# A state-space scan beside a mixture of experts: GpSimd adds the sums of two steps in every second pair of steps of blocks 1 to 4, and TensorE sums four states at once there

## The chip, the core and the metric

The kernel runs on one core of a Trainium2 chip. Its time is the device time of one execution in microseconds (us); for the kernel before the change it is 1565.81 us, the median of three runs. A core has a matrix engine (TensorE, PE in the profile, with PEld for its weight loads), three engines for element-wise work (VectorE or DVE, ScalarE or ACT, GpSimd or POOL), an engine that here issues the transfers (SyncE, SP), and 16 DMA engines. Each engine takes its own instructions in the order in which the program gives them, and waits at an instruction until the semaphores that it needs have come.

## The reference

`x` has 2 sequences of 2048 tokens of 256 channels. It is layer-normed (`xn`), and the output is `x + s * g`:

- `s` is a Mamba layer with residual, then an MLP with residual. Of `xn` (rms-normed) an input projection makes `xp` and `z`, 512 channels each; a causal convolution over 4 tokens and a silu make `xc`; `dt = softplus(...)`, `B` and `C` (16 values per token each) are projections of it. Then the scan over the tokens, for each of 512 channels and 16 states:

```python
def step(h, ts):
    dt_t, B_t, C_t, u_t = ts
    dA = jnp.exp(dt_t[..., None] * A)
    h = h * dA + (dt_t * u_t)[..., None] * B_t[:, None, :]
    y = jnp.einsum('bds,bs->bd', h, C_t)
    return (h, y)
```

  and `(y + xc * D) * silu(z)` goes through the output projection.
- `g` is the silu of a mixture of experts: a gate picks 2 of 8 experts for each token, each expert is 256 to 1024 (relu) to 256.

The change is in the `einsum`: for every channel and token, the 16 products `h * C` are summed over the states.

## The kernel before

Everything is in 32-bit floats. The 4096 tokens are cut into 8 blocks of 512 (`T`), four to a sequence; the 512 channels into 4 groups `d` of 128 partitions; the 16 states into 8 pairs `g`. One **step** `n` (0 to 255, `at[n] = (c, d, g)`, so block `c` is `n // 32` and pair `g` is `n % 8`) does two states of one channel group of one block:

- ScalarE makes `da`, the two exponentials of `dt` times A, two steps ahead (`exps`, L1238).
- VectorE multiplies `du` by the pair's B (L1345) and runs two scans along the 512 tokens (L1349) into the tile `h`, 128 x 2 x 512, one of five buffers. At the first pair of a group it makes `du` (L1342).
- ScalarE saves the last token's state for the next block (`save`, L1275), one step later.
- GpSimd multiplies `h` by the pair's C in place, both states in one instruction of 1024 elements a partition (`times_c`, L1279). For nearly all steps (`paired`) it then adds the second state to the first (L1281).
- TensorE sums over the states: `accumulate` multiplies the identity by the 128 x 512 tile and adds it into the PSUM tile `y` of the channel group (L1251). A `paired` step needs one such matmul, others two. The first matmul of a group adds `xc * D` by a diagonal matrix (L1247). A matmul of 32-bit floats appears as two records in the profile. After the last pair VectorE multiplies `y` by the gate (`gated`, L1259).

The order of all this is written out by hand. In the loop of step `n` the scan of `n` is followed by `save` and `times_c` of `n - 1`, the exponentials of `n + 2`, then `sums(n - LAG)` with `LAG` 3, which calls `accumulate`. After that comes `draw(HALF + owed)`: it takes pieces of other work from lists, until 2.0 us of TensorE time by the planner's own costs (0.86 for a matmul of 512 columns) are given out, twice in each step. The sums are not counted in it. The other work is: the expert and MLP tiles (`Ffn.run`: matmuls L854 and L866, transposes L844, activation L954 on ScalarE, sum L966 on VectorE), the front of the next block (`front`: projections L557, L602, L621, convolution L567 to L582), the gate projection (L708) and the output projection (`out_proj`, L762). In blocks 1 to 4 these are expert tiles.

Inside `front` lies the chain that makes the next block's `dt`, for two channel groups at a time, twice per block: matmuls L621, five activations on ScalarE (L629 to L635), one subtraction on GpSimd (L636), a logarithm on ScalarE (L643), then a subtraction and an add on GpSimd (L648, L649). Beside the first logarithm, `root` makes the norm factors of an earlier block: GpSimd L800, ScalarE L802 and L803, GpSimd L227 to L230. All of these stand in the engines' ordinary queues between the steps' own instructions.

Of the kernel before, what the change touches and what calls it, by code (L numbers as in the profile page):

```python
# [11 lines left out]
ALU = mybir.AluOpType  # L12
# [37 lines left out]
def kernel(  # L50
# [18 lines left out]
    nc = tc.nc  # L69
# [303 lines left out]
    def ring(tag, bufs):  # L373

        n = take(tag)
        later.free(tag, n - bufs)
        return tag, n
# [818 lines left out]
    hs, ys, y_n, hts, das, dus = {}, {}, {}, {}, {}, {}  # L1196
# [45 lines left out]
    def accumulate(n):  # L1242
        c, d, g = at[n]
        if g == 0:
            y_n[c, d] = ring("y", 1)
            ys[c, d] = ps_1.tile([P, T], F32, tag="y", name=f"y{c}_{d}")
            nc.tensor.matmul(ys[c, d], ddiag[:, d, :], xcs[c, d], start=True, stop=False)  # L1247
            skips[0] += 1
        nq = 1 if paired(n) else 2
        for q in range(nq):  # L1250
            nc.tensor.matmul(  # L1251
                ys[c, d], ident, hts[n][:, q, :], start=False,
                stop=(g == DS // 2 - 1 and q == nq - 1),
            )
        if g == DS // 2 - 1:
            y, sz, twice = ys[c, d], szs[c, d], 1.0 if d else 0.5

            def gated():
                nc.vector.scalar_tensor_tensor(sz, y, twice, sz, ALU.mult, ALU.mult)  # L1259
                y_made.add((c, d))  # L1260

            later.put(gated, y_n[c, d], after=2)

    def sums(n):

        g = at[n][2]
        if g:
            if g == 1:
                accumulate(n - 1)
            accumulate(n)  # L1270
# [6 lines left out]
    def times_c(n):  # L1277
        c, d, g = at[n]
        nc.gpsimd.tensor_tensor(hts[n], hts[n], bct[c, "C", g], ALU.mult)  # L1279
        if paired(n):  # L1280
            nc.gpsimd.tensor_tensor(hts[n][:, 0, :], hts[n][:, 0, :], hts[n][:, 1, :], ALU.add)  # L1281

    def paired(n):

        return n >= 8 and not (n >= 190 and n % 2 == 0)
# [34 lines left out]
    for n in range(NS):  # L1320
# [15 lines left out]
        for q in range(2):  # L1336
# [17 lines left out]
            if q == 0 and n > 0:  # L1354
                save(n - 1)
                times_c(n - 1)
# [9 lines left out]
            owed = draw(HALF + owed)  # L1366
    save(NS - 1)
    times_c(NS - 1)
    for n in range(NS - LAG, NS):
        sums(n)  # L1370
# [63 lines left out]
```

## Time and profile before

| | |
|---|---|
| runs | 1567.42, 1560.62, 1565.81 us, median 1565.81 |
| the profiled execution | 1572.91 us, of which span 1571.2 us |
| granted TensorE clock, mean | 0.94 |
| TensorE matmul busy | 1401.4 us, 89% of the span |
| VectorE busy | 1247.6 us, 79% |
| GpSimd busy | 1157.2 us, 74% |
| ScalarE busy | 920.1 us, 59% |
| step 32 starts (its multiply by B, L1345) | 280.7 us |
| step 160 starts | 946.7 us |
| sums L1251 | 594 matmul records, median 592 ns |

The profile shows one execution. A busy time is the time in which an engine runs its instructions. The time in which it stands idle before an instruction is put down to what released that instruction. A group line gives line, engine, operation, the tiles written and read, shapes and count, then busy time and mean duration, then idle time before and who ended it. A timeline line gives start, duration, engine, line, operation and count. "L" is a line of the kernel as printed above. Busy time of TensorE is modelled with overlapping matmuls, so the distance between starts says more of its pace than the duration does.

### The profile page before, as it was taken

To read this page: it belongs to the slowest core of one execution; us is meant where nothing else is said; L and a number is where in the kernel's file an instruction comes from. 1 tells how busy PE (TensorE), PEld (TensorE's weight loads), DVE (VectorE), ACT (ScalarE), POOL (GpSimd) and SP (SyncE) were. 2 spreads that over 40 slices of the span, in tenths; PEclk is the share of its full clock that TensorE was granted. 3 is DMA by queue.
4 is the path that set the end of the run, shared out by engine and by line. 5 is a ranking of instruction groups with operands and counts; after the bars stand their busy time and mean duration, and the time that the engine had idled before them with its cause. 6 is when DMAs were issued, how large, how long until landed. Compare 5 with 4: busy or idle time off the path is not lost. (4 is left out here: it accounts for less than half of the span.)

```text
span 1571.2 us, 18477 instructions
## 1 busy us (share of the span) xinstructions
PE 1401.4 (89%) x5246; PEld 985.5 (63%) x5246; DVE 1247.6 (79%) x1362; ACT 920.1 (59%) x1890; POOL 1157.2 (74%) x775
## 2 busy tenths in 40 slices
PE   5745999998999999999999999999898898799767
PEld 3532667765776667667776777667555565567536
DVE  7458898798778977799879777996898696899952
ACT  4735576567655755477657665675566564374423
POOL 2668589867886689679967887688866768677852
PEclk8557999999999999999999999999999989899988
DMA  5576335923494347724763368245832437645312
GB/s 190 187 258 252 111 120 182 327 91 102 141 321 146 96 131 250 256 88 132 234 255 110 118 213 295 87 127 180 314 105 87 143 101 249 214 131 164 96 59 84
DMA packets 203749, 265.17 MB, mean 169 GB/s; under 512 B 21744, under 2 KB 174192, under 8 KB 203648
## 3 DMA queue, kind: packets, MB, share of 16 engines
q1 hardware_dynamic: 197504, 247.21, 48.0%
q0 software_dynamic: 6144, 16.79, 3.2%
q8 instruction: 42, 0.69, 0.2%
q14 instruction: 59, 0.48, 0.1%
HBM read 227.50 MB, written 36.44 MB: 168 GB/s over the span
## 5 line engine op out<-in xcount | busy, mean ns | idle before, releaser
L1279 POOL TENSOR_TENSOR h<-h,C 128x1024 f32<-128x1024 f32 x256 | 609.9, 2384 | 246.3 <-ACT hs L1275 193.9
L1349 DVE TENSOR_TENSOR_SCAN h<-da,hs,b 128x512 f32<-128x512 f32 x384 | 479.7, 1271 | 42.6 <-PE y L1251 17.2
L1238 ACT ACTIVATE da<-dt,a_neg 128x512 f32<-128x512 f32 x512 | 358.0, 718 | 40.3 <-DVE h L1349 39.7
L1251 PE MATMUL y<-h,ident 128*128 128x512 f32 x594 | 304.6, 615 | 30.6 <-POOL h L1279 20.2
L1345 DVE TENSOR_TENSOR b<-du,B 128x1024 f32<-128x1024 f32 x256 | 314.8, 1230 | 18.0 <-DMA B<-bcd 11.1
L854 PE MATMUL phe<-xsTe,w_e 128*128 128x256 f32 x1248 | 290.4, 384 | 12.5 <-ACT hide L954 8.8
L1281 POOL TENSOR_TENSOR h<-h 128x512 f32<-128x512 f32 x215 | 277.9, 1292 | 16.9
L854 PEld LDWEIGHTS phe<-xsTe,w_e 128*128 128x128 f32 x1248 | 238.7, 192 | 80.6 <-issue 26.3
L866 PE MATMUL poe<-w_e,hide 128*128 128x256 f32 x1248 | 288.7, 380 | 0.0
L866 PEld LDWEIGHTS poe<-w_e,hide 128*128 128x128 f32 x1248 | 235.7, 190 | 64.9 <-issue 33.6
L954 ACT ACTIVATE hide<-phe,b 128x256 f32<-128x256 f32 x312 | 129.3, 469 | 128.9 <-PE phe L854 128.7
L1251 PEld LDWEIGHTS y<-h,ident 128*128 128x128 f32 x594 | 113.0, 197 | 119.6 <-issue 63.3
L1349 DVE TENSOR_TENSOR_SCAN h<-da,b 128x512 f32<-128x512 f32 x128 | 151.3, 1211 | 11.1 <-PE y L1251 3.2
L854 PE MATMUL phm<-xsTm,w_m 128*128 128x256 f32 x512 | 130.9, 410 | 22.7 <-DVE hidm L1015 19.9
L854 PEld LDWEIGHTS phm<-xsTm,w_m 128*128 128x128 f32 x512 | 104.1, 205 | 55.0 <-DVE hidm L1015 24.2
L866 PE MATMUL pom<-w_m,hidm 128*128 128x256 f32 x512 | 119.0, 384 | 2.0 <-DVE xom L1086 1.7
L866 PEld LDWEIGHTS pom<-w_m,hidm 128*128 128x128 f32 x512 | 97.7, 193 | 28.6 <-issue 11.0
L459 POOL DMA_INDIRECT xs_d<-xt,slot x64 | 63.9, 998 | 49.8 <-issue 22.2
L1275 ACT COPY hs<-h 128x2 f32<-128x2 f32 x192 | 36.1, 188 | 94.7 <-DVE h L1349 92.3
L1042 POOL DMA_INDIRECT ykm<-ys_d,row_y x64 | 61.4, 960 | 38.9 <-issue 11.7
L1015 DVE SCALAR_TENSOR_TENSOR hidm<-hidm,phm 128x512 f32<-128x512 f32 x64 | 42.7, 671 | 55.6 <-ACT hidm L1013 55.6
L582 DVE SCALAR_TENSOR_TENSOR xc<-px,par_sb,xc 128x512 f32<-128x512 f32 x96 | 71.5, 747 | 17.2 <-ACT xc L574 11.8
(175 smaller groups left out, 1431.6 us busy)
## 6 DMA issues: line engine op xcount, KB each, us to landing
w_e<-in_w SPq DMA_DIRECT2D x312, 256.0 KB
B<-bcd SPq DMA_DIRECT2D x64, 512.0 KB
C<-bcd SPq DMA_DIRECT2D x64, 512.0 KB
w_m<-in_mlp_w1T SPq DMA_DIRECT2D x64, 256.0 KB
w_m<-in_mlp_w2T SPq DMA_DIRECT2D x64, 256.0 KB
xs<-xs_d SPq DMA_DIRECT2D x39, 256.0 KB
ys_d<-ys SPq DMA_DIRECT2D x39, 256.0 KB
b<-in_b SPq DMA_DIRECT2D x39, 128.0 KB
```

Of the source, the lines that this page charges most:

```text
L459: r = nc.gpsimd.indirect_dma_start(out=xs_d, out_offset=bass.IndirectOffsetOnAxis(ap=slot[:, k, i : i + 1], axis=0), in_=x_of(i // J, i % ...
L582: nc.vector.scalar_tensor_tensor(v[:, s : s + T], px, conv_w[:, d, KC - 1 - s : KC - s], v[:, s : s + T], ALU.mult, ALU.add,)
L854: nc.tensor.matmul(ph[:, q, :], self.w1[c0 // 2][:, k, ts(q, P)], self.xT[:, k, :], start=(k == 0), stop=(k == KM - 1),)
L866: nc.tensor.matmul(po[:, j, :], self.hid[c // 2][:, c % 2, ts(j, P)], self.w2[c // 2][:, c % 2, :], start=(c == 0 and j == 0), stop=(c == ...
L954: nc.scalar.activation(hc[:, q, :], ph[:, q, :], AF.Relu, bias=self.b1[:, c0 + q : c0 + q + 1])
L1042: nc.gpsimd.indirect_dma_start(out=yk[k][:, j, :], out_offset=None, in_=ys_d, in_offset=bass.IndirectOffsetOnAxis(ap=row_y[:, k, i0 + j : ...
L1238: nc.scalar.activation(das[n][:, q, :], dts[c, d], AF.Exp, scale=a_neg[:, d, 2 * g + q : 2 * g + q + 1])
L1251: nc.tensor.matmul(ys[c, d], ident, hts[n][:, q, :], start=False, stop=(g == DS // 2 - 1 and q == nq - 1),)
L1279: nc.gpsimd.tensor_tensor(hts[n], hts[n], bct[c, "C", g], ALU.mult)
L1281: nc.gpsimd.tensor_tensor(hts[n][:, 0, :], hts[n][:, 0, :], hts[n][:, 1, :], ALU.add)
L1345: nc.vector.tensor_tensor(inp, dus[c, d].unsqueeze(1).to_broadcast([P, 2, T]), bct[c, "B", g], ALU.mult,)
L1349: nc.vector.tensor_tensor_scan(hts[n][:, q, :], das[n][:, q, :], inp[:, q, :], 0.0 if c % CPB == 0 else hs[c - 1][:, d, 2 * g + q : 2 * g ...
```

## The change

In steps 32 to 159 (blocks 1 to 4) with `n % 4 == 3`, GpSimd gets one more add of 128 x 512: the pair sum of step `n - 1` is added onto the pair sum of step `n`. TensorE then makes no matmul for step `n - 1` (`nq` is 0), and its matmul for step `n` sums four states at once. There are 32 such steps. `n` and `n - 1` always belong to the same channel group, and neither is the group's first pair.

```diff
@@ accumulate(n)
-        nq = 1 if paired(n) else 2
+
+        nq = 0 if fours(n + 1) else 1 if paired(n) else 2
         for q in range(nq):
             nc.tensor.matmul(
                 ys[c, d], ident, hts[n][:, q, :], start=False,
@@ times_c(n)
         nc.gpsimd.tensor_tensor(hts[n], hts[n], bct[c, "C", g], ALU.mult)
         if paired(n):
             nc.gpsimd.tensor_tensor(hts[n][:, 0, :], hts[n][:, 0, :], hts[n][:, 1, :], ALU.add)
+        if fours(n):
+            nc.gpsimd.tensor_tensor(
+                hts[n][:, 0, :], hts[n][:, 0, :], hts[n - 1][:, 0, :], ALU.add
+            )
+
+    def fours(n):
+
+        return 32 <= n < 160 and n % 4 == 3
```

## The prediction

> **What bounds the kernel now.** I read the page first (busy rows and slices), then the busy times of the four stretches in which blocks 1 to 4 are scanned, since only steps 32 to 159 change. Columns: stretch, its us, then busy time (and instructions) of TensorE, weight loads, VectorE, ScalarE, GpSimd; granted clock; DMA.
>
> ```profile
> 280.00:452.00 172.00, 162.84 (x630) 116.58 (x629) 139.32 (x127) 106.96 (x234) 134.56 (x83) 0.99 0.55 175
> 452.00:621.00 169.00, 160.69 (x622) 114.75 (x621) 137.69 (x127) 104.71 (x227) 131.97 (x82) 0.99 0.52 168
> 621.00:783.00 162.00, 159.79 (x630) 115.44 (x629) 138.44 (x127) 102.17 (x190) 136.42 (x84) 1.00 0.57 186
> 783.00:946.00 163.00, 159.12 (x623) 114.13 (x622) 135.87 (x128) 105.51 (x229) 130.43 (x81) 1.00 0.55 178
> ```
>
> TensorE is busy 642.4 of 666 us, with no more than 23.6 us idle; GpSimd 533.4, so 132.6 idle; VectorE 551.3. A step takes 666/128 = 5.20 us, while VectorE alone, in steps with no wait, goes from one multiply by B to the next in 3.73 to 3.85 us (timeline). So TensorE sets the pace and the other three wait for it.
>
> The rows of the two groups that the edit touches on GpSimd, from the page (count, busy us, mean ns, idle before):
>
> ```profile
> L1279 POOL TENSOR_TENSOR h<-h,C 128x1024 f32<-128x1024 f32 x256 | 609.9, 2384 | 246.3 <-ACT hs L1275 193.9
> ...
> L1281 POOL TENSOR_TENSOR h<-h 128x512 f32<-128x512 f32 x215 | 277.9, 1292 | 16.9
> ```
>
> And TensorE's own timeline, for what a sum costs (start, us, instruction):
>
> ```profile
> 316.08 1.02 PE L1251 MATMUL y<-h,ident 128*128 128x512 f32 x2
> 316.94 1.88 PE L557 MATMUL px<-xrTr,in_sb 128*128 128x512 f32 x4
> ```
>
> One sum of one 128x512 tile is two matmul records, and the next work starts 316.94 - 316.08 = 0.86 us after it, not 1.02 and not 2 x 0.592. Last, the waits inside 280 to 960 us (us in total, times, longest):
>
> ```profile
> POOL h L1279 <- ACT hs L1275: 97.1, 47, 6.3
> ...
> ACT rms L802 <- POOL rms L800: 9.7, 4, 4.4
> PEld y L1251 <- POOL h L1281: 9.5, 8, 3.1
> POOL h L1279 <- DVE h L1349: 8.9, 5, 3.3
> PE phe L854 <- ACT hide L954: 8.8, 3, 4.5
> ```
>
> GpSimd mostly waits for ScalarE's save of the last state. But TensorE also waits for GpSimd at a few places (its y matmuls 5.6 us in 4 waits, in the same view filtered to TensorE), and ScalarE waits for it too.
>
> **What the change removes.** Of 128 steps, those with n % 4 = 2 lose their sum: 32 x 0.86 = 27.5 us of TensorE time. Every one lies on the engine that sets the pace, so 27.5 us is the gain if nothing else moves. Here a page of the Trainium skill bears on it: "Perfetto Trace Analysis", Identifying the Most-Contended Engine, says that TensorE's matmul occupancy is no measure of headroom because matmuls are pipelined, and that weight-load busy share should be used. Weight loads are busy 460.9 of 666 us, 69%, below VectorE's 83%: by that reading VectorE is the contended engine and the removal gains about nothing. By occupancy, 64 records of 0.592 would be worth 37.9 us. The start spacing lies between: eight matmuls of 256 columns take 1.72 us here and two of 512 take 0.86, back to back, while weight loads hide between them. I take 27.5.
>
> **What it adds.** 32 adds of 128x512 on GpSimd, in steps n % 4 = 3, after the add of the step's own two states. The trace has the same shape at L1281: 1.27 us median, 1.29 mean; so 41 us on GpSimd, whose idle time in the four blocks is 132.6. Where GpSimd waits for ScalarE before its next multiply, the add costs nothing. Where it doesn't, all behind it in its queue is 1.27 us later: the multiplies by C and the first adds, the three operations of the step-size chain (L636, L648, L649) and the root of the norm (L800, L227 to L230). No DMA is issued on GpSimd in these blocks.
>
> No instruction changes its place on any other engine, SP's queue included. Two releases move. The sum of a step n % 4 = 3 now waits for one add more; queued behind it on TensorE are that half step's expert and projection matmuls, for which ScalarE (L954) and VectorE (L966) wait. And the state buffer of the step before is freed by that add instead of a matmul; the scan that reuses it is four steps after the add. At n = 59 GpSimd ends at 446.3 and scan 63 starts at 449.0, the narrowest margin that I found, 2.8 us; 1.27 fits, so nothing for this. If that cover is gone, the scan waits up to about 1 us in VectorE's slack.
>
> A second rule speaks against the change: "SBUF — State Buffer", Who interferes with whom, says that a VectorE operation with two inputs in SBUF and a GpSimd operation that reads SBUF exclude each other for a whole instruction. L1342 (du) is of that kind: 672 ns at best, 951 median in the blocks, so the trace shows such waiting. GpSimd's busy share rises by 41/666, 6 points. If each of the 17 du in the blocks then met a full 1.27 us add that often, that is 17 x 0.06 x 1.27 = 1.3 us of VectorE time; without the rule nothing. VectorE has 115 us idle there, so I take zero for the path, 1.3 at worst.
>
> **Where the adds come onto the path.** I compared, step by step in the timeline, when GpSimd ends with step n and when the sum of n starts. Mostly TensorE is 3 to 15 us behind GpSimd. The margin goes away only after the step-size chain of the next block, twice in each block. Block 1, first time:
>
> ```profile
> 374.44 2.37 POOL L1279 TENSOR_TENSOR h<-h,C 128x1024 f32<-128x1024 f32 x1 [4.78 <-ACT hs L1275]
> ...
> 376.89 1.27 POOL L1281 TENSOR_TENSOR h<-h 128x512 f32<-128x512 f32 x1
> 378.12 2.51 POOL L636 TENSOR_TENSOR ls<-ls,ex 128x512 f32<-128x512 f32 x2
> ...
> 384.24 0.20 POOL L800 TENSOR_SCALAR rms<-rms 128x4 f32<-128x4 f32 x1
> 384.48 0.20 ACT L802 ACTIVATE rms<-rms 128x4 f32<-128x4 f32 x1 [4.42 <-POOL rms L800]
> ...
> 386.83 3.54 PE L854 MATMUL phe<-xsTe,w_e 128*128 128x256 f32 x8 [4.48 <-ACT hide L954]
> ```
>
> This is step 47, n % 4 = 3: its new add lands at 378.1, ahead of L636 and L800. ScalarE stands at L802, and behind it in its queue stand L643, the exponentials for VectorE (L1238) and the activation of the expert (L954), for which TensorE waits 4.48 us. So this add is paid in full, 1.27, and the sum taken out of TensorE at step 46 only makes its wait longer, 0.86: 2.13 us against the ideal.
>
> Going through all such places (margin before the change):
> - Block 1: step 47 as shown, 2.13. Steps 55 and 57, margin 0.05 each, TensorE waiting 0.28 and 2.29: one add in that run, 2.13. Sum 4.3.
> - Block 2: step 79, the same chain, TensorE waiting 3.46: 2.13. Steps 87 and 89, margins 0.92 and 0.05: 2.13. Sum 4.3.
> - Block 3: GpSimd runs from step 112 to 127 without idling, so the adds pile up. Step 113, margin 0.87: 1.26; step 115, margin 2.60 against two adds: 0.4; step 123, margin 5.23 against four: 1.6. Sum 3.3.
> - Block 4: step 145, margin 0.05: 2.13; step 147 (1.90): 0.2; step 153 (1.09): 1.0; step 155 (2.83): 0.4. Sum 3.8 with rounding.
>
> Together 15.7 us, so 27.5 - 15.7 = 11.8 remains. TensorE also has waits of 1 to 2 us for other engines (for L557, L602, L762), behind which a removed sum only makes the wait longer; I charge two sums, 1.7. Gain 10.1, called 10. After step 159 the code is the same and its waits are relative to each other, so the 10 us should last to the end.
>
> **The sum.** The profiled execution took 1572.9 (span 1571.2 and 1.7 around it); 1572.9 - 10 = 1562.9. The median of the runs, 1565.8, is 7.1 below the profiled one; less 10 that is 1556.
>
> **Rivals.**
> - *The adds hide nearly everywhere.* For it: 97 us of GpSimd's waiting for ScalarE in the blocks. Against it: the root at steps 47 and 79, where there is no gap to hide in. If only those two are paid, 27.5 - 4.3 = 23 gained: 1543.
> - *VectorE and ScalarE come next.* TensorE's step would shrink to 4.98 us, VectorE needs 3.8 plus its other work (83% busy), and ScalarE's queue is in order. Small waits of TensorE of 0.05 us per step over 128 steps would take 6 of the 10: 1562. For it: 23.6 us of idle that TensorE has already. Against it: VectorE's pace when not held.
> - *GpSimd becomes the bound in the step-size stretches (slower).* An add that is on the path costs 2.13 with the sum it replaces, so the change loses as soon as 27.5/2.13 = 13 of the 32 adds are on it. I count about 7.4. Block 3 shows how it would go: GpSimd never idles for 16 steps, lags, delays L636, L800 and L649, ScalarE stands behind them and starves VectorE and the experts. Were it so in all four blocks with 5 adds each, 20 x 2.13 - 27.5 = +15: 1581. Against it: after each such stretch GpSimd regains 3.2 to 6 us within a few steps, since its multiply and add take 3.66 us against the 5.2 of a step; with the new add 3.98 on average, still below.
>
> **How the numbers follow.** About 0.5% (7.8 us: below 1558.0, above 1573.6) can be told from no change here. Likeliest, 1552 to 1559: 0.44. Adds hidden, 1541 to 1551: 0.15. Eaten by VectorE and ScalarE, 1559 to 1566: 0.23. GpSimd on the path, 1570 up to 1581: 0.18. Faster: 0.38 of the first and 0.15, 0.53. Slower: 0.15 of the last. Same: the rest, 0.32. The range 1545 to 1571 leaves out about 0.05 below and 0.15 above.
>
> **What would show it.** Right: y matmuls from 594 records to 530; 32 more GpSimd adds near 1.27 us; the wait of GpSimd for the save of the state smaller by most of 41 us; the four blocks shorter by about 10 us in all with TensorE's idle time up from 23.6 to about 40; the two long waits at L802 near 5.7 instead of 4.42. Wrong: the blocks shorter by 20 or more (my margins were too strict), or TensorE's waits for y or for L954 grown by more than 25 us (the slower rival). A difference that arises after 960 us would contradict the step that carries the gain to the end.

## The result and the profile after

The changed kernel takes 1573.79 us (median of nine runs, 1571.02 to 1577.40) against 1561.19 for the kernel before in the same nine rounds: ratio 1.0087, 95% interval 1.0062 to 1.0112. It is slower; the forecast was 10 us faster, with a range of 1545 to 1571 us.

The first 160 us differ between the profiles, whatever the kernel: step 32 starts at 280.7 us in the profile before, at 270.2 in the one after, and between 265 and 290 in those below. So everything from here on is compared by the **stretch**: from the multiply by B of step 32 to that of step 168, in one profile each (168, because the lines that trail behind step 160 have closed up by then). It is 709.2 us before and 723.2 after: 14.0 us longer. After step 168 the two traces run in parallel, the difference moving by 0.4 us until the end. The loss arose in blocks 1 to 4. Two kernels below that should not differ are 0.5 us apart in the stretch, so differences of that size are not read.

The busy times in blocks 1 to 4, from step 32 to step 160, after the change (columns as in the prediction's first view):

```profile
270.20:954.10 683.90, 634.65 (x2465) 457.60 (x2464) 549.97 (x505) 421.63 (x886) 576.38 (x360) 0.98 0.54 173
```

TensorE stands idle 49.3 us of 683.9, where it was 23.6 of 666. Its work did get shorter, so something else holds it. The waits between 270 and 960 us, longest first:

```profile
POOL h L1280 <- ACT hs L1276: 74.9, 38, 5.1
ACT hide L954 <- PE phe L854: 65.8, 45, 7.7
DVE h L1358 <- POOL h L1284: 65.4, 7, 12.5
ACT hs L1276 <- DVE h L1358: 62.2, 30, 5.8
```

and two lines of the corresponding view before (280 to 960 us):

```profile
ACT hs L1275 <- DVE h L1349: 24.7, 14, 3.8
DVE h L1349 <- PE y L1251: 19.2, 8, 5.5
```

L1358 is the scan (L1349 before), L1280 the multiply by C, L1282 the add within a step, L1284 the new add, L1252 the sum, L1276 the save. The third line is new: in seven places VectorE's scan waits for the new add, 65.4 us together, up to 12.5 at once. The fourth follows from it: ScalarE's save waits 62.2 us for scans, where it was 24.7 us before. From the groups of the page before, then after:

```profile
L1349 DVE TENSOR_TENSOR_SCAN h<-da,hs,b 128x512 f32<-128x512 f32 x384 | 479.7, 1271 | 42.6 <-PE y L1251 17.2
...
L1358 DVE TENSOR_TENSOR_SCAN h<-da,hs,b 128x512 f32<-128x512 f32 x384 | 479.5, 1271 | 81.5 <-POOL h L1284 42.0
```

In the whole trace VectorE's idle time before these scans (384 of the 512) went from 42.6 to 81.5 us, and its chief releaser from TensorE to GpSimd. One such place in the timeline, first the scan of step 61 before the change, then steps 59 to 61 after it:

```profile
436.82 1.28 DVE L1349 TENSOR_TENSOR_SCAN h<-da,hs,b 128x512 f32<-128x512 f32 x1 [1.27 <-PE y L1251]
```

```profile
436.71 0.73 ACT L1238 ACTIVATE da<-dt,a_neg 128x512 f32<-128x512 f32 x1
437.27 1.27 POOL L1282 TENSOR_TENSOR h<-h 128x512 f32<-128x512 f32 x1
...
438.62 1.27 POOL L1284 TENSOR_TENSOR h<-h,h 128x512 f32<-128x512 f32 x1
...
439.93 1.28 DVE L1358 TENSOR_TENSOR_SCAN h<-da,hs,b 128x512 f32<-128x512 f32 x1 [12.03 <-POOL h L1284]
...
443.01 0.19 ACT L1276 COPY hs<-h 128x2 f32<-128x2 f32 x1 [2.82 <-DVE h L1358]
```

The add at 438.62 is that of step 59. The scan that starts 0.04 us after it ends is that of step 61: two steps on, not four. It waits for its output buffer. The step 59 add is the last reader of the tile of step 58, so step 61 has been given the buffer of step 58, three steps back. In the built program the buffer addresses show it: the five buffers of `h` were each reused after exactly 5 steps before the change; after it, of the 128 steps 32 to 159, 75 reuse a buffer after 5 steps, 33 after 6, 7 after 4 and 13 after 3. No line of the diff names a buffer. The tile of a step n with n % 4 = 2 is now released by an instruction that stands earlier in the program: the add, in the loop of step n + 2, instead of the matmul, in the loop of step n + 3, where the scan of n + 3 stands ahead of it. The allocation then gives such a tile's buffer out before older ones. The addresses fit an order of release: at each of the 13 places the two next scans get theirs after 6 steps, at each of the 7 the next one does. Why it happens at 20 of the 32 steps and not at the others was not looked into.

### The profile page after: what moved, and what is told of

Same layout as the page of the kernel before. It is cut to its first block, busy times and chain, and to the rows that moved or that the text cites. A ratio compares the mean times of both kernels' runs of the same rounds, so it can differ in the third digit from the quotient of the medians.

```text
span 1575.1 us, 18350 instructions
## 1 busy us (share of the span) xinstructions
PE 1386.1 (88%) x5182; PEld 974.7 (62%) x5182; DVE 1248.3 (79%) x1362; ACT 919.5 (58%) x1890; POOL 1197.2 (76%) x807
## 5 line engine op out<-in xcount | busy, mean ns | idle before, releaser
L1280 POOL TENSOR_TENSOR h<-h,C 128x1024 f32<-128x1024 f32 x256 | 610.8, 2387 | 218.7 <-ACT hs L1276 171.8
L1358 DVE TENSOR_TENSOR_SCAN h<-da,hs,b 128x512 f32<-128x512 f32 x384 | 479.5, 1271 | 81.5 <-POOL h L1284 42.0
L1354 DVE TENSOR_TENSOR b<-du,B 128x1024 f32<-128x1024 f32 x256 | 314.8, 1230 | 19.3 <-DMA B<-bcd 13.1
L854 PE MATMUL phe<-xsTe,w_e 128*128 128x256 f32 x1248 | 293.8, 388 | 22.5 <-ACT hide L954 14.6
L1252 PE MATMUL y<-h,ident 128*128 128x512 f32 x530 | 274.9, 623 | 38.8 <-POOL h L1280 21.3
L1282 POOL TENSOR_TENSOR h<-h 128x512 f32<-128x512 f32 x215 | 277.1, 1289 | 16.9
L1252 PEld LDWEIGHTS y<-h,ident 128*128 128x128 f32 x530 | 101.3, 199 | 128.9 <-issue 63.0
L1358 DVE TENSOR_TENSOR_SCAN h<-da,b 128x512 f32<-128x512 f32 x128 | 151.1, 1210 | 32.1 <-POOL h L1284 23.4
L1276 ACT COPY hs<-h 128x2 f32<-128x2 f32 x192 | 36.1, 188 | 139.9 <-DVE h L1358 139.5
L866 PEld LDWEIGHTS pom<-w_m,hidm 128*128 128x128 f32 x512 | 97.8, 193 | 28.7 <-issue 10.8
L1015 DVE SCALAR_TENSOR_TENSOR hidm<-hidm,phm 128x512 f32<-128x512 f32 x64 | 42.6, 670 | 56.1 <-ACT hidm L1013 56.1
L582 DVE SCALAR_TENSOR_TENSOR xc<-px,par_sb,xc 128x512 f32<-128x512 f32 x96 | 71.5, 746 | 15.7 <-ACT xc L574 12.3
```

The source lines that it names most:

```text
L582: nc.vector.scalar_tensor_tensor(v[:, s : s + T], px, conv_w[:, d, KC - 1 - s : KC - s], v[:, s : s + T], ALU.mult, ALU.add,)
L854: nc.tensor.matmul(ph[:, q, :], self.w1[c0 // 2][:, k, ts(q, P)], self.xT[:, k, :], start=(k == 0), stop=(k == KM - 1),)
L866: nc.tensor.matmul(po[:, j, :], self.hid[c // 2][:, c % 2, ts(j, P)], self.w2[c // 2][:, c % 2, :], start=(c == 0 and j == 0), stop=(c == ...
L1252: nc.tensor.matmul(ys[c, d], ident, hts[n][:, q, :], start=False, stop=(g == DS // 2 - 1 and q == nq - 1),)
L1354: nc.vector.tensor_tensor(inp, dus[c, d].unsqueeze(1).to_broadcast([P, 2, T]), bct[c, "B", g], ALU.mult,)
L1358: nc.vector.tensor_tensor_scan(hts[n][:, q, :], das[n][:, q, :], inp[:, q, :], 0.0 if c % CPB == 0 else hs[c - 1][:, d, 2 * g + q : 2 * g ...
```

## The experiments

Two theories stood against each other. **A**: the early reuse takes VectorE's lead away and costs the time. **B**: the adds' own time on GpSimd does, through the step-size chain and ScalarE's queue. Stretches, us:

| kernel | stretch | ratio to before (95%) |
|---|---|---|
| before | 709.2 | |
| changed | 723.2 | 1.0087 (1.0062 to 1.0112) |
| before_ring: before, buffers tied | 709.7 | 1.0012 (0.9998 to 1.0027) |
| after_ring: changed, buffers tied | 711.7 | 1.0038 (1.0026 to 1.0050) |
| ring_skip: tied, sums left out, no adds | 699.0 | 0.9925 (0.9897 to 0.9953) |
| ring_add: tied, adds, all sums | 721.3 | 1.0117 (1.0087 to 1.0147) |
| free_skip: as ring_skip, not tied | 698.4 | 0.9924 (0.9901 to 0.9948) |
| away: changed, 24 adds, not tied | 712.7 | 1.0031 (1.0015 to 1.0046) |
| ring_away: away, tied | 702.2 | 0.9962 (0.9949 to 0.9976) |
| ring_fed: after_ring, planner fed | 723.3 | 1.0153 (1.0122 to 1.0184) |
| ring_away_fed: ring_away, planner fed | 709.9 | 0.9925 (0.9899 to 0.9951) |
| ring_skip2: as ring_skip, 64 sums left out | 690.9 | 0.9893 (0.9857 to 0.9929) |

**The buffers.** "Tied" is this edit, with the same for the eight tiles that use the buffers ahead of the scan:

```diff
-hts[n] = work.tile([P, 2, T], F32, tag="h", name=f"h{c}_{d}_{g}")
+hts[n] = work.tile([P, 2, T], F32, tag=f"h{(n + NBLK) % 5}", name=f"h{c}_{d}_{g}", bufs=1)
```

before_ring, the control:

> The kernel before, with the five state buffers tied to the step by hand (step n takes buffer (n + 8) % 5, as it did already). Both theories: nothing changes, ratio 1.000 within 0.3%. It is the control for the next three, which use the same tying.

As expected; the stretch agrees within 0.5 us. after_ring:

> The changed kernel with each state buffer reused after exactly 5 steps, as before the change, instead of after 3, 4 or 6. Theory A (early reuse: a scan two steps after the new add takes the buffer that this add gives back and waits for it, so VectorE loses its lead): VectorE's 65 us of waits for the new add fall below 5 us, the stretch of steps 32 to 159 becomes 5 to 15 us shorter than before the change instead of 14.0 longer, ratio 0.990 to 0.997. Theory B (the adds' own time on GpSimd delays the step-size chain and, through ScalarE's queue, TensorE): nothing of the loss goes away, ratio 1.007 to 1.010, stretch 12 to 15 us longer.

Between the two. With nothing changed but the buffers, 11.5 us of the stretch go away (723.2 to 711.7; 2.7, 2.6, 3.0 and 3.2 in the four blocks, taken to the steps 72, 104, 136 and 168), and the intervals of the ratios of changed and after_ring lie apart. VectorE's waits for the new add fall from 65.4 to 0.8 us, and ScalarE's save waits 29.9 us for scans. What is left among the scan's long waits is the one that it had before:

```profile
DVE h L1358 <- PE y L1252: 20.7, 9, 5.4
```

Scan 61 starts here at 429.99 us, 12.8 us ahead of its own multiply by C on GpSimd. Before the change this lead was 13.1 us; in the changed kernel, where the scan has to wait until GpSimd is done with step 59, it is 3.6. So A is shown, with 11.5 us. But the promised gain does not come back: the kernel is still 2.0 us longer in the stretch than before_ring. Something else is wrong with the forecast as well.

**The two halves of the trade.** ring_skip removes the add and keeps the removal of the sum:

```diff
-        if fours(n):
-            nc.gpsimd.tensor_tensor(
-                hts[n][:, 0, :], hts[n][:, 0, :], hts[n - 1][:, 0, :], ALU.add
-            )
```

> As the last, but without the new adds: TensorE leaves out the sums of the steps n % 4 = 2 and GpSimd does no more than before, so those states are missing from the output. It prices the removed matmuls alone. Both theories: 32 x 0.86 = 27.5 us at most; with TensorE's other waits taking some of it, the stretch is 20 to 27 us shorter, ratio 0.983 to 0.988. If it is shorter by less than 10, TensorE was not what sets the pace.

It brings 10.7 us (709.7 to 699.0), well under the 20 to 27 expected. The busy times from step 32 to step 160, of before_ring and then of ring_skip:

```profile
265.80:932.30 666.50, 643.00 (x2498) 461.25 (x2497) 551.03 (x505) 419.69 (x880) 533.10 (x327) 0.99 0.55 177
270.00:927.00 657.00, 621.73 (x2438) 451.78 (x2438) 550.62 (x505) 419.65 (x881) 532.07 (x326) 0.98 0.56 179
```

TensorE idles 23.5 us in the first and 35.3 in the second. I added up its gaps over the whole stretch from the distances between matmul starts, which unlike busy time leave the pipelining out: about 35 us in before_ring, 52 in ring_skip. So 16.8 of the 27.5 us came back as waiting: some 6 more for VectorE, as much for ScalarE, none for GpSimd, and 4 to 5 with no releaser found. ring_add does the reverse: its add writes the second half of the tile, which nothing reads any more, and TensorE makes all sums.

```diff
-        nq = 0 if fours(n + 1) else 1 if paired(n) else 2
+        nq = 1 if paired(n) else 2
...
-                hts[n][:, 0, :], hts[n][:, 0, :], hts[n - 1][:, 0, :], ALU.add
+                hts[n][:, 1, :], hts[n][:, 0, :], hts[n - 1][:, 0, :], ALU.add
```

> The kernel before with the tied buffers and the 32 new adds, whose result goes into the second half of the step's tile, which nothing reads any more; TensorE makes all its sums as before. It prices the adds alone. Theory A: 32 x 1.27 us mostly hidden, about 1.27 us for each of some 7 to 8 places on the path, so the stretch is 5 to 12 us longer, ratio 1.003 to 1.008. Theory B: at least 14 + 20 = 34 us longer, ratio 1.02 or more.

11.6 us longer (709.7 to 721.3), inside the 5 to 12 that A expected for the stretch, though its ratio, 1.0117, is above the 1.003 to 1.008 named with it. On top of ring_skip the adds cost 711.7 - 699.0 = 12.7. Both ways round the price of the adds is 12 us, and B in its strong form falls.

**Does early reuse cost by itself?** free_skip is ring_skip without the tying.

> The sums of steps n % 4 = 2 left out, no new adds (those states are missing from the output), and the buffers not tied: buffers are then reused after 3 and 6 steps all through blocks 1 to 4, and after 2 steps twice. With tied buffers the stretch took 699.0. Theory A in its wide form (early reuse costs by itself): 704 to 712 us, and VectorE waits for GpSimd for 20 us or more. In its narrow form (it costs only when the late new add is what gives the buffer back): 699 to 702 us.

By its addresses 24 scans in the four blocks get a buffer after 3 steps, more than in the changed kernel, and the scan does wait for it (L1354 is the scan here, L1282 the add within a step):

```profile
DVE h L1354 <- POOL h L1282: 43.1, 8, 7.1
```

Yet the stretch is 698.4 against 699.0. VectorE waited 43 us at no cost: the buffer is given back by the add within step n % 4 = 2 itself, earlier than the new add would be, none of the waits is above 7.1 us, and scan 61 keeps a lead of 7.4 us. So early reuse by itself does not cost. I then thought that early reuse hurts only where the step-size chain makes the add late, and moved the adds away from it:

```diff
-        return 32 <= n < 160 and n % 4 == 3
+        return 32 <= n < 160 and n % 4 == 3 and n % 32 not in (15, 23)
```

away, with that edit on the changed kernel:

> 24 adds (not in the steps n % 32 = 15 and 23), buffers not tied, so reused after 3 steps in many places. With tied buffers the stretch took 702.2. If early reuse hurts only behind a late add, and the adds are late only in the step-size chain, 702 to 706 us; if it hurts at every new add, 709 to 714.

A miss. It takes 712.7, and 702.2 when tied, so early reuse costs 10.5 us here too, though no new add stands directly ahead of the chain any more. By the addresses the same 13 scans get a buffer after 3 steps as in the changed kernel, so the edit left the cause in place. The scan's waits are as long as in the changed kernel:

```profile
DVE h L1358 <- POOL h L1284: 70.5, 8, 11.8
```

They stand at the same steps (61, 85, 101, 117, 125, 149, 157, and now 53). GpSimd is late there from the chain's own operations, and the add that gives the buffer back comes after them: ahead of scan 61 GpSimd works without a gap from 411.7 us to the end of that add at 436.6, of which 5.2 us are L648 and L649. ring_away, the same with tied buffers:

> The changed kernel with tied buffers, but the steps n % 32 = 15 and 23, whose add stands ahead of the step-size chain on GpSimd, keep the two-matmul form without a new add (24 adds instead of 32). So far, from step 32 to step 168: 709.7 us with tied buffers alone, 699.0 with the sums left out and no add, 711.7 with both. If the adds cost where the step-size chain is late (the prediction's places), 24 adds cost 3 to 5 us instead of 12.7 and the stretch is 704 to 707 us, ratio 0.995 to 0.999. If each add costs alike wherever it is, 24/32 of both: 711.2 us.

702.2, below even the 704 to 707 expected from the places: the eight adds in front of the chain, a quarter of all, carry 9.5 us of after_ring's stretch (711.7 to 702.2), net of eight sums that TensorE does again. That is 2.8, 2.6, 1.9 and 2.2 us in the four blocks, or 1.2 us for each of these adds even after the sum that it saves. This version is faster than the kernel before, ratio 0.9962.

**Where the removed sums' time goes.** ring_fed lets the planner give TensorE 0.86 us of other work in the half step that lost its sum:

```diff
-            owed = draw(HALF + owed)
+            fed = MM if q == 0 and fours(n - LAG + 1) else 0.0
+            owed = draw(HALF + fed + owed)
```

> The changed kernel with tied buffers; in the half step whose sum is left out the planner gives TensorE 0.86 us more of other work. Theory C (the sums' time came back as short waits for VectorE and ScalarE, because a step without its sum is over before they hand on): the stretch lengthens towards 715 us, but expert work moves ahead by up to 27.5 us and the end comes sooner than the stretch says: ratio 0.993 to 1.000 against 1.0038 unfed. Rival (the waits are VectorE's own pace, whatever TensorE is given): no gain over unfed, 1.003 to 1.006.

> Both of the last two edits. By theory C and the places: 0.985 to 0.996, faster than the kernel before. By their rivals: 1.002 to 1.006.

The two contradict each other. ring_away_fed ends at 0.9925, inside theory C's range, the fastest kernel here that computes everything, with a stretch of 709.9 and the time regained after step 216. ring_fed ends at 1.0153, outside both forecasts, and falls back both in the stretch and, by some 15 us, around step 180. Feeding changes the order of all later work, so neither says much about theory C; it stays open why one gains and the other loses.

ring_skip2 leaves out twice as many sums, and has no adds:

```diff
-        return 32 <= n < 160 and n % 4 == 3
+        return 32 <= n < 160 and n % 2 == 1
```

> Tied buffers, no new adds, and twice as many sums left out: every even step of blocks 1 to 4, 64 sums, 55 us of TensorE (those states are missing from the output). The first 32 shortened steps 32 to 168 from 709.7 to 699.0 us, 10.7 of the 27.5 that they took. If VectorE's and ScalarE's pace is what comes next, the second 32 bring less than the first: 691 to 697 us. If each removed sum is worth the same wherever it is, about 688. If the first were lost to a few fixed places only, the second bring more than the first, 680 us or less.

690.9: the second 32 bring 8.1 us, a little less than the first. It lies at the edge of the first forecast and not far from the second, so it decides little. Relieving the other engines tells more. Relief of VectorE is the first edit, relief of ScalarE the second, each on before_ring (all sums) and on ring_skip:

```diff
-                for s in range(1, KC):
+                for s in range(1, 2):
...
-                nc.scalar.activation(ls, ex, AF.Identity, bias=1.0)
-                nc.scalar.activation(ls, ls, AF.Identity, bias=minus1)
-                later.put(lambda: engine(d).tensor_tensor(ls, ls, ex, ALU.subtract))
+                later.put(lambda: engine(d).tensor_tensor(ls, ex, ex, ALU.subtract))
```

> The kernel before with tied buffers, VectorE doing one convolution tap (L582) of three for each channel group, so 2 x 0.75 us less for each of 16 groups in the four blocks, 24 us of VectorE (two taps are missing from the convolution). Control for the next. As TensorE sets the pace before the change, little: 705 to 709 us against 709.7.

> The same relief of VectorE, with the 32 sums left out and no new adds (two taps and those states missing from the output). If VectorE's pace took the removed sums' time, the removal is now worth 16 to 25 us against the control instead of 10.7. If the time is lost on hand-overs that do not hang on VectorE's load, still 9 to 12.

> Control: the kernel before with tied buffers, ScalarE without the two activations L634 and L635 of each channel group in the step-size chain, some 1.3 us x 16 = 21 us less in the four blocks (the small correction of the softplus is left out). Stretch of steps 32 to 168: 700 to 708 us against 709.7, since the chain that TensorE waits for twice a block is shorter too.

> The same relief of ScalarE, the 32 sums left out and no new adds (correction and those states missing from the output). If ScalarE's queue takes the removed sums' time, the removal is worth 15 us or more against actrel; if not, 9 to 12 as without relief.

> Control with both reliefs (two convolution taps and the correction missing): 695 to 703 us.

> Both reliefs and the 32 sums left out, no new adds. If the two engines' loads explain the loss, the removal is worth 20 us or more against bothrel; if the loss lies in hand-overs whatever the loads, 14 to 17.

| | all sums | 32 sums left out | worth of the removal |
|---|---|---|---|
| no relief | 709.7 | 699.0 | 10.7 |
| VectorE relieved | 704.5 | 689.9 | 14.6 |
| ScalarE relieved | 688.7 | 676.7 | 12.0 |
| both | 681.8 | 663.3 | 18.5 |

All in the stretch's us; the ratios to before are 0.9893 (relief), 0.9808 (relief_skip), 0.9848 (actrel), 0.9760 (actrel_skip), 0.9769 (bothrel) and 0.9629 (bothrel_skip), the last four from two runs each. The controls came out shorter than expected, most of all those with ScalarE relieved (688.7 against 700 to 708, 681.8 against 695 to 703). The removal's worth fell between the two forecasts with VectorE relieved and with both, and at the edge of the lower one with ScalarE relieved. With less work on both engines it is 18.5, not 20 as I had set, and not 27.5. So relieving VectorE and ScalarE gives back 7.8 of the 16.8 us that are lost; the relief of ScalarE also shortens the step-size chain, and load and chain are not separated here. The other 9 stay open: they could be hand-overs, from the end of one engine's instruction to the start of the next engine's, whose length does not hang on load, but no run isolates them.

A sixth state buffer, which might let VectorE keep more of its lead, doesn't fit: of the 64 KB per partition that the tiles of B and C need, 62 would be left. No run has one.

## Why the prediction was wrong, point by point

The forecast for the stretch was -27.5 + 15.7 + 1.7 = -10.1 us; measured it is +14.0. The 24.1 us between them are 11.5 for the buffers, 10.8 for the removal, 1.3 for the adds and 0.5 in the tied control. Either of the first two is by itself more than the whole gain forecast.

- **The release of the state buffer: "so nothing for this".** This step failed, and it is the largest term. It took for granted that a buffer comes round after five steps, as all do before the change. It asked whether the add is done four steps on, and it is; but 13 scans were given the buffer two steps after the add. Forecast 0, measured 11.5. The prediction had also bounded it by "about 1 us in VectorE's slack". The waits are up to 12.5 us. As I read it, VectorE's lead over GpSimd, five buffers deep, was what bridged the step-size chain, and it is cut down at just those steps: at scan 61 it is 13.1 us before, 3.6 after and 12.8 tied, and 7.4 in free_skip, where nothing is lost. How much lead is needed was not measured.
- **The removal: "I take 27.5".** This term failed too. The cost of a sum is right: 0.86 us between starts, and it is gone. But the sum charged only 1.7 us for other waits, plus about 4.3 at the places where TensorE waits for GpSimd (0.86 each at steps 47, 55, 79, 87 and 145), so -21.5. Measured alone: -10.7, or 1.0, 2.0, 4.2 and 3.4 us in the four blocks, each of which lost 6.9 us of sums. Of the 16.8 us that came back as waits, some 12 are put down to VectorE and ScalarE. The rival "VectorE and ScalarE come next" named it with 6 us; the removal fell short of the forecast by 10.8. TensorE idled 23.6 of 666 us before the change, which I read as a bound on what the others take; but it does not show how soon the others are late once TensorE goes faster.
- **The adds.** Forecast 15.7 with those 4.3 of lost sums in it, so 11.4; measured 11.6 (ring_add) and 12.7 (on top of ring_skip). The sum is right. At the place that the forecast showed it is close too: TensorE's wait behind the root of block 1 was 4.48 us, and in the changed kernel it is

```profile
377.55 3.62 PE L854 MATMUL phe<-xsTe,w_e 128*128 128x256 f32 x8 [6.33 <-ACT hide L954]
```

  1.85 more, and 2.20 more in block 2 (3.46 to 5.66), where 2.13 was said. But block by block it is not: without the lost sums the forecast is 2.6, 2.6, 3.3 and 2.9 us, ring_add shows 3.5, 5.4, 0.3 and 2.4, and after_ring against ring_skip 0.4, 3.6, 3.4 and 5.3. That the sums agree so well is in part luck. The check named for L802 was wrong, too: the wait there stays 4.41 at the two places, because ScalarE itself arrives 1.3 us later, held at L643, whose wait for L636 goes from 1.34 to 2.67 us.
- **The weight-load rule** (the Trainium skill, "Perfetto Trace Analysis", Identifying the Most-Contended Engine), by which the removal was put at nothing: 10.7 us lie between that and the 27.5 of the start spacing, and so do the 18.5 with the other engines relieved. The page names a second measure beside the weight-load share, MFU (the share of the peak rate of arithmetic), which the prediction left out; so only the share, taken alone, is contradicted here.
- **The shared-port rule** (the Trainium skill, "SBUF — State Buffer", Who interferes with whom): the trace shows the exclusion. From the timeline before:

```profile
365.63 2.35 POOL L1279 TENSOR_TENSOR h<-h,C 128x1024 f32<-128x1024 f32 x1
...
367.35 1.19 DVE L1342 TENSOR_TENSOR du<-dt,xc 128x512 f32<-128x512 f32 x1
```

  GpSimd's multiply ends at 367.98, and du, which started in the middle of it, 0.56 us later. So it goes for 13 of the 17 du in the blocks before the change: each starts while a GpSimd instruction runs and ends 0.55 to 0.56 us after it. The other four take 0.67 to 0.68 us. With the 32 adds the 17 du take 17.7 us in all instead of 16.6 (median 910 ns, 951 before). This 1.0 us lies inside the 1.3 at worst; that it reached the path isn't shown.
- **To the end**: right; 0.4 us of difference arises after step 168.

## What to carry to other kernels

An edit that changes which instruction is the last to read a tile also changes when its buffer is free in program order, and the allocation may hand out other buffers than before: compare the buffer addresses of both builds, or tie them to the step, before costing anything else. A removed instruction on the busiest engine need not be worth its full time: here 10.7 of 27.5 us, and most of the rest came back as waits for two engines that are busy 83% and 63%. And an add put on an engine with 20% of idle time still costs nearly in full where a chain through that engine's queue is what the others wait for (1.2 of 1.27 us for each of the eight adds in front of the chain), so choose its steps by the chain.

## What the runs showed that was not expected

Leaving out two activations on ScalarE (0.63 and 0.72 us) in the step-size chain, in 16 channel groups, some 21 us of work on an engine that is busy 63% of the time, shortened the stretch by 21.0 us (709.7 to 688.7). Two taps of VectorE work for as many groups, 24 us on an engine that is busy 83%, shortened it by 5.2. That the 21.0 equal the length of the work is chance: 18.1 of them arise in blocks 1 and 2, none in block 3 and 2.9 in block 4. In blocks 1 and 2 lie TensorE's long waits behind the root. The one that the prediction shows with 4.48 us is in actrel, at the same matmul (L852 there):

```profile
384.60 1.99 PE L852 MATMUL phe<-xsTe,w_e 128*128 128x256 f32 x8 [1.13 <-ACT hide L952]
```

So what counted was where TensorE waits for the chain, more than how busy an engine is.
